# A graph network kernel on one core: constant products in TensorE's pauses, the first load in halves, the last group finished in pairs

## The chip, the core and the metric

The kernel runs on one core of a Trainium2 chip. A core has five engines that run their own instruction streams in order and meet at semaphores: TensorE (PE in the profile; its weight loads are the row PEld), VectorE (DVE), ScalarE (ACT), GpSimd (POOL) and SyncE (SP), which here only issues DMAs. The metric is device time in microseconds (us) of one execution; lower is better. The kernel before took 2499.52 us, the median of three runs (2499.09 to 2500.66).

## The reference

The inputs are x, 128 graphs ("batches") of 128 nodes with 256 features, and adj, their 128x128 adjacency matrices. Four layers follow each other, each wrapped as `x = layernorm(x + layer(x, adj))`:

- Layer 0 is a gated graph network of three steps. A step computes `m = h @ weight[i]`, sums the messages over the graph, `aggr = adj^T @ m`, and updates the state with a GRU cell: `gi = aggr @ w_ih.T + b_ih`, `gh = h @ w_hh.T + b_hh`, two sigmoid gates, one tanh candidate.
- Layers 1, 2 and 3 are graph attention: `Wh = x @ W.T`, scores `e[i,j] = leaky(a1.Wh[i] + a2.Wh[j])`, masked by adj, softmax over j, and `out = attention @ Wh`. Layer 2 gives 0 where a row has no neighbour.

All of it is float32.

## The kernel before

**Tiling.** The 128 batches are taken in 32 groups of 4 (`G = 4`, `NG = 32`). A tile has 128 partitions; the state of a group is two tiles of 128 features by 512 columns (4 batches of 128 nodes). `gru(g, stage)` (L675) does layer 0 for group g, `gat(g, ...)` (L838) the three attention layers.

**Layer 0.** The products of the GRU cell are done in Strassen's form with seven block products per gate pair (`strassen`, L631); its matmuls (L649) accumulate in five PSUM banks with the tag "gate". They multiply tiles with two constant weight tables: `whs`, made from w_hh, and `wcs[i]`, made at the start of each step's first use from `weight[i]` and w_ih (`input_weights`, L452: matmuls at L465, evictions by `scale`, seven block sums L429 to L435). All other PSUM results go through three banks with the tag "bank". For groups 0 and 1 the input is transposed by TensorE (`transposed`, L546, matmuls L554); for later groups by DMA (`turned`, L500: a copy that splits 32-bit words into 16-bit halves, L404 or L406, a DMA transpose L516, and a copy that joins them, L510). Steps 1 and 2 split the state into three bfloat16 parts (`thirds`, L521, subtractions at L536).

**Attention layers.** Scores are dot products on VectorE with an accumulator (L850); masked rows with their maximum at L885; leaky ReLU, exp and row sums on ScalarE (L889, L906); the attention matrix is transposed and multiplied (L956), evicted, and multiplied by the weights (L967); L973 adds the residual on VectorE, one instruction per batch, two batches per PSUM bank. The layernorm of these layers is `deviation` (L586): per batch a square with a sum on ScalarE (L590), then one small VectorE instruction for all four batches (L594 in the first attention layer, L601 later), then `power` (L560), a GpSimd instruction that raises 128x4 numbers to -0.5 (L563). After the last layer four ScalarE instructions scale the four batches (L980) and one DMA of 512 KB writes the group out (L982).

**What sets the order.** The program is unrolled. A planner (`Plan`, L51) gets every operation with assumed durations per engine that may do it (for instance `{"ACT": 475, "DVE": 602}`), its reads and writes, a priority by group and stage, and the pools of buffers; it places operations one after the other by a list schedule, repeats this with due times worked back from the result (`latest`, L125), seven passes in all, and keeps the pass with the shortest planned span (`order`, L102). It decides the order on each engine, which engine does an operation that may run on two or three, and the buffer slot. `LATER` (L342) shifts the stages of different groups against each other, so that layer 0 of some groups runs beside the attention of others; the last four groups (`LAST = 4`, "the tail") are done by priority alone, and use TensorE transposes instead of DMA ones. Because of the planner a change of one operation can move instructions far away from it.

**The start.** VectorE zeroes three small tiles "f" (L369), which later hold scores. SP issues the loads in this order: x of group 0 (xs, 512 KB, L681), its adj (am, 256 KB, L682), weight[0] (256 KB), w_ih (2 x 384 KB, L424), x of group 1 (512 KB), w_hh (2 x 384 KB), adj of groups 1 to 4, and x of group 2, which takes over the buffer of group 0's x. TensorE does, in this order: 8 transposes of group 0's x, 16 products with its adj (L719), 4 transposes of group 1's x, the products for `wcs[0]` (L465), 4 more, and then the gate products.

Of the kernel before, what the change touches and what calls it, by code (L numbers as in the profile page):

```python
# [16 lines left out]
P = 128  # L17
# [291 lines left out]
def adj_resnorm_kernel(  # L309
# [30 lines left out]
    U16, BF16 = mybir.dt.uint16, mybir.dt.bfloat16  # L340
    BOTH = ("DVE", "POOL")
    LATER = (0.25, 1.75, -0.5, -0.25, 0.25, -1.0)  # L342
    plan = Plan({t: n for t, (n, _) in tags.items()}, own)
# [24 lines left out]
    for t in slots["f"]:  # L368
        nc.vector.memset(t, 0.0)  # L369

# [31 lines left out]
    def copy(e, dst, src):  # L402
        if e == "ACT":
            nc.scalar.copy(dst, src)  # L404
        else:
            nc.vector.tensor_copy(dst, src)  # L406
# [138 lines left out]

    def transposed(src, src_of, prio):  # L546

        res = []
        for c in range(KC):
            b_, dst = bank(), Buf("k2", GN)  # L550

            def fn(e, b_=b_, c=c):
                for b in range(G):
                    nc.tensor.transpose(T(b_)[:, b * P:(b + 1) * P], src_of(b, c), ident)  # L554
            plan.op({"PE": 437}, fn, reads=[src], writes=[b_], prio=prio)
            plan.op(EVICT, lambda e, b_=b_, dst=dst: copy(e, T(dst), T(b_)), reads=[b_], writes=[dst], prio=prio)
            res.append(dst)
        return res

    def power(ve, prio):  # L560

        rstd = Buf("v", G)
        plan.op({"POOL": 980}, lambda e: nc.gpsimd.tensor_tensor(T(rstd), T(ve), neghalf, ALU.pow),  # L563
                reads=[ve], writes=[rstd], prio=prio, port=BOTH, holds=False)
        return rstd
# [19 lines left out]

    def deviation(y, before, prio):  # L586

        ss, ve = Buf("v", G), Buf("v", G)
        for b in range(G):
            plan.op({"ACT": 400}, lambda e, b=b: nc.scalar.activation(  # L590
                next(nobody[0]), T(y)[:, b, :], AF.Square, accum_out=T(ss)[:, b:b + 1]),
                reads=[(y, b)], writes=[(ss, b)], prio=prio, lag=85)
        if before is None:
            plan.op({"DVE": 78}, lambda e: nc.vector.tensor_scalar(  # L594
                T(ve), T(ss), 1.0 / D, EPS, op0=ALU.mult, op1=ALU.add),
                reads=[(ss, b) for b in range(G)], writes=[ve], prio=prio, port=BOTH)
        else:
# [3 lines left out]
            plan.op({"DVE": 78}, lambda e: nc.vector.scalar_tensor_tensor(  # L601
                T(ve), T(ss), 1.0 / D, T(eps), op0=ALU.mult, op1=ALU.add),
                reads=[(ss, b) for b in range(G)] + [eps], writes=[ve], prio=prio, port=BOTH)
        return ve
# [26 lines left out]
    def strassen(gates, kept, prio):  # L631
# [41 lines left out]
        return o0, o1, bx  # L673

    def gru(g, stage):  # L675

# [16 lines left out]
        if g < 2:  # L693
            hT = transposed(xs, lambda b, c: T(xs)[:, b, c * P:(c + 1) * P], prio)
# [8 lines left out]
        for i in range(STEPS):  # L703
# [4 lines left out]
            for c in range(KC):  # L708
# [11 lines left out]
                if by_thirds and h is not None:  # L720
                    plan.op({"PE": 12 * 55.6 + 56}, fn, reads=[low, h[0][c], h[0][2]], writes=[b_], prio=prio, room=[a_, t])
                else:
                    plan.op({"PE": 4 * 222.7}, fn, reads=[am, xs if h is None else h[c]], writes=[b_], prio=prio, room=[a_, t])
                agg.append(a_)
# [113 lines left out]
    def gat(g, xc, no, stage):  # L838
# [3 lines left out]
        for l in range(3):  # L842
# [118 lines left out]
            for b0 in range(0, G, 2):  # L961
# [9 lines left out]
                for b in (b0, b0 + 1):  # L971
# [4 lines left out]
                            reads=[b_, rden, (xc, b)], writes=[(y, b)], prio=prio)  # L976
            xc, ve = y, deviation(y, ve, prio)
            rstd = power(ve, prio)
        for b in range(G):
            plan.op({"ACT": 400}, lambda e, b=b: nc.scalar.mul(T(xc)[:, b, :], T(xc)[:, b, :], T(rstd)[:, b:b + 1]),  # L980
                    reads=[(xc, b), rstd], writes=[(xc, b)], prio=prio)
        plan.op({"SP": 60}, lambda e: nc.sync.dma_start(out[g * G:(g + 1) * G].rearrange("b n d -> n b d"), T(xc)),  # L982
                reads=[(xc, b) for b in range(G)], prio=prio)

# [57 lines left out]
```

## Time and profile before

| | |
|---|---|
| runs | 2499.09, 2499.52, 2500.66 us |
| the profiled execution | 2499.94 us, of which the instructions span 2497.9 us |
| instructions in the profile | 42545 |
| TensorE busy | 2469.1 us, 99% |
| VectorE busy | 2164.0 us, 87% |
| ScalarE busy | 1925.7 us, 77% |
| GpSimd busy | 781.9 us, 31% |
| share of 16 DMA engines that the main queue used | 29.9% |
| mean granted TensorE clock | 0.997 |

The profile is of one execution. "Busy" of TensorE has modelled ends: a matmul is given its whole latency (0.38 us for 128 columns by 256), while the next one starts 0.216 us after it, so a busy TensorE may still have lost time between two starts. Rows of the timeline read: start, length, engine, line, operation, output<-inputs, shapes, count, and in brackets how long the engine was idle before and what ended that. Rows of a window read: from and to, its length, the busy time of each engine with its number of instructions, the granted TensorE clock (1.00 is full speed), the share of the DMA engines and GB/s. Where the profile has no record of the clock the row shows 1.00.

### The profile page before, as it was taken

The numbers are of one execution on the slowest core, as the hardware profiler recorded it, in microseconds if no ns is written. First come the engines' busy times: TensorE is split into PE (matmuls) and PEld (weight loads), VectorE is DVE, ScalarE is ACT, GpSimd is POOL, SyncE is SP. The second block draws the span as 40 slices with busy tenths as digits, with TensorE's granted clock in tenths as the row PEclk, the third lists the DMA queues.
The fourth block names the chain that finished last, engine by engine and source line by source line (L and its number), as shares of the span: only waits on it lengthen the run. The fifth ranks groups of instructions, "written<-read, shape, count | busy, mean of one in ns | idle before, by whom it ended". The sixth has DMA issues, their size and how long they took to land.

```text
span 2497.9 us, 42545 instructions
## 1 busy us (share of the span) xinstructions
PE 2469.1 (99%) x13492; PEld 2180.1 (87%) x13492; DVE 2164.0 (87%) x6461; ACT 1925.7 (77%) x4835; POOL 781.9 (31%) x999
## 2 busy tenths in 40 slices
PE   8999999999999999999999999999999999999998
PEld 7888888888888888888888888888888888888877
DVE  6789888989888988889988889988889988877797
ACT  6578777888778787788887778887787888666577
POOL 2232233422334332334333334233333332211001
PEclk9999999999999999999999999999999999999999
DMA  5223233233333332333242233333233333110101
GB/s 148 56 56 64 60 76 69 64 81 60 76 64 73 72 81 60 73 68 73 68 77 68 61 80 68 73 71 74 60 77 68 76 65 68 26 39 18 38 1 35
DMA packets 456609, 161.38 MB, mean 65 GB/s; under 512 B 389184, under 2 KB 454720, under 8 KB 456384
## 3 DMA queue, kind: packets, MB, share of 16 engines
q1 hardware_dynamic: 455952, 158.65, 29.9%
q8 instruction: 106, 1.74, 0.3%
q14 instruction: 119, 0.97, 0.1%
q10 hardware_dynamic: 432, 0.01, 0.0%
HBM read 45.89 MB, written 16.78 MB: 25 GB/s over the span
## 4 chain that ended last, share of the span: by engine, by line
PE 86%; DVE 6%; ACT 4%; DMA 2%; issue 1%; POOL 0%; POOLq 0%; ACTq 0%; DVEq 0%
PE gate L649 63%; PE bank L967 10%; PE bank L956 6%; PE bank L716 3%; PE bank L719 2%; DVE nobody L850 2%; DMA k<-k 1%; DVE k L973 1%; ACT k L906 1%; ACT k L404 1%; DMA xs<-in_x_dram 1%; ACT k L510 1%; DVE k L406 1%; DVE k L654 1%; PE bank L822 0%
## 5 line engine op out<-in xcount | busy, mean ns | idle before, releaser
L649 PE MATMUL gate<-k,whs 128*128 128x256 f32 x4032 | 1205.2, 381 | 3.5 <-ACT k L742 1.6
L649 PE MATMUL gate<-k,wcs 128*128 128x256 f32 x4032 | 1199.3, 379 | 1.3 <-ACT wcs L404 1.3
L649 PEld LDWEIGHTS gate<-k,wcs 128*128 128x128 f32 x4032 | 766.0, 190 | 105.8 <-ACT wcs L404 1.8
L649 PEld LDWEIGHTS gate<-k,whs 128*128 128x128 f32 x4032 | 741.2, 190 | 107.8 <-ACT k L742 9.6
L654 DVE TENSOR_TENSOR k<-gate,k 128x512 f32<-128x512 f32 x576 | 388.4, 685 | 125.6 <-PE gate L649 80.4
L563 POOL TENSOR_TENSOR v<-v,neghalf 128x4 f32<-128x4 f32 x128 | 159.3, 1244 | 843.5 <-DVE v L601 460.9
L967 PE MATMUL bank<-gwT,k 128*128 128x256 f32 x1536 | 349.6, 380 | 1.6 <-DVE k L406 0.8
L967 PEld LDWEIGHTS bank<-gwT,k 128*128 128x128 f32 x1536 | 290.1, 190 | 43.7 <-DVE k L406 3.6
L850 DVE SCALAR_TENSOR_TENSOR nobody<-k,wa 128x256 bf16<-128x256 f32 x768 | 297.7, 427 | 0.7 <-ACT k L582 0.7
L753 ACT ACTIVATE k<-k,brz 128x256 f32<-128x256 f32 (+1 forms) x384 | 229.6, 624 | 71.1 <-DVE k L654 71.0
L618 POOL TENSOR_TENSOR k<-k,k 128x256 f32<-128x256 f32 x272 | 232.9, 867 | 104.1 <-DVE k L792 37.9
L404 ACT COPY k<-bank 128x512 f32<-128x512 f32 (+1 forms) x272 | 155.1, 572 | 112.0 <-PE bank L956 56.3
L735 ACT COPY k<-gate 128x512 f32<-128x512 f32 x288 | 167.9, 584 | 87.2 <-PE gate L649 83.7
L536 POOL TENSOR_TENSOR k<-k 128x512 f32<-128x512 f32 (+1 forms) x143 | 155.9, 1090 | 239.1 <-DVE k L792 189.4
L404 ACT COPY k<-k 128x512 bf16<-128x512 bf16 (+1 forms) x265 | 175.7, 694 | 53.8 <-DVE k L792 27.3
L869 POOL PARTITION_BROADCAST k<-k x336 | 138.4, 512 | 240.3 <-DVE k L406 149.1
L590 ACT ACTIVATE nobody<-k 128x256 bf16<-128x256 f32 x384 | 157.0, 415 | 60.5 <-DVE k L973 60.3
L510 ACT COPY k<-k 128x1024 uint16<-128x1024 uint16 x163 | 189.9, 1166 | 17.1 <-DMA k<-k 15.2
L956 PEld LDWEIGHTS bank<-k,k 128*128 128x128 f32 x1536 | 183.8, 192 | 11.0 <-DVE k L918 3.7
L956 PE MATMUL bank<-k,k 128*128 128x128 f32 x1536 | 190.2, 277 | 2.4 <-ACT k L510 1.5
L782 ACT ACTIVATE k<-k,bi 128x512 f32<-128x512 f32 x192 | 136.6, 726 | 66.4 <-DVE k L779 52.5
L973 DVE SCALAR_TENSOR_TENSOR k<-bank,v,k 128x256 f32<-128x256 f32 x384 | 166.9, 476 | 23.0 <-PE bank L967 22.8
(110 smaller groups left out, 3296.7 us busy)
## 6 DMA issues: line engine op xcount, KB each, us to landing
xs<-in_x_dram SPq DMA_DIRECT2D x32, 512.0 KB, 3.9
k<-in_x_dram SPq DMA_DIRECT2D x32, 512.0 KB, 4.1
out_dram<-k SPq DMA_DIRECT2D x32, 512.0 KB, 2.9
am<-in_adj_dram SPq DMA_DIRECT2D x32, 256.0 KB, 4.2
k<-k SPq DMA_TRANSPOSE x366, 3.1
k<-in_gnn_wT_dram SPq DMA_DIRECT2D x3, 256.0 KB, 4.7
k<-in_w_ihT_dram SPq DMA_DIRECT2D x2, 384.0 KB, 5.7
k<-in_w_hhT_dram SPq DMA_DIRECT2D x2, 384.0 KB, 6.7
```

Source lines behind the costliest of these rows:

```text
L404: nc.scalar.copy(dst, src)
L510: nc.scalar.copy(flat().bitcast(U16).rearrange("p (q h) -> p q h", h=2), T(rows).bitcast(U16).rearrange("p (h q) -> p q h", h=2))
L563: plan.op({"POOL": 980}, lambda e: nc.gpsimd.tensor_tensor(T(rstd), T(ve), neghalf, ALU.pow), reads=[ve], writes=[rstd], prio=prio, port=B ...
L618: nc.vector if e == "DVE" else nc.gpsimd).tensor_tensor(T(t)[:, j, :], a(), b(), ALU.subtract),
L649: nc.tensor.matmul(T(dst)[:, j * H:(j + 1) * H], T(w)[:, m, gt, :], moving(m, ms)[1](), start=first and n == 0, stop=n == len(todo) - 1, s ...
L654: plan.op({"DVE": 602}, lambda e: nc.vector.tensor_add(T(o)[:, :, j * H:(j + 1) * H], T(b_).rearrange("p (g n) -> p g n", g=2), T(part).re ...
L735: plan.op({"ACT": 475}, lambda e: nc.scalar.copy(T(dst), T(src)), reads=[src], writes=[(dst, 0), (dst, 1)], prio=prio)
L753: nc.scalar.activation(T(o)[:, gt, n0:n1], src(), AF.Tanh, bias=brz[:, gt * KC + c:gt * KC + c + 1], scale=0.5)
L850: plan.op({"DVE": 345}, lambda e, b=b, h=h, l=l, side=side, xc=xc: nc.vector.scalar_tensor_tensor(next(nobody[1]), T(xc)[:, b, :], 1.0, T( ...
L956: nc.tensor.matmul(T(b_)[:, b * P:(b + 1) * P], T(xc)[:, b, c * P:(c + 1) * P], T(pT)[:, b, :], start=True, stop=True)
L967: nc.tensor.matmul(T(b_)[:, (b - b0) * D:(b - b0 + 1) * D], T(aT[k])[:, b * P:(b + 1) * P], T(gwT)[:, l, k, :], start=(k == 0), stop=(k == ...
L973: nc.vector.scalar_tensor_tensor(T(y)[:, b, :], T(b_)[:, (b - b0) * D:(b - b0 + 1) * D], T(rden)[:, b:b + 1], T(xc)[:, b, :], op0=ALU.mult ...
```

## The change

There are four parts.

1. **Eight products at the start.** The tiles "f" are filled with 1.0 instead of 0.0, and before anything else TensorE multiplies the first of them with itself eight times (`idle_product`, 128x128 float32) into a gate bank. Nobody reads the result.
2. **Products in planned pauses.** After planning, the kernel walks over TensorE's operations in planned order. Where the plan has a pause of more than 1200 ns and there is a gate bank with no user left, it puts one or more such products ahead of the next operation: (pause - 1200) / 437 rounded down, plus one. In the built program that makes three places, all after the last gate product: four products ahead of the first transpose L822, three more behind it, and one ahead of the last pair of L956.
3. **The first x in halves.** For group 0 the load of x is two DMAs of two batches (256 KB) each, and `transposed` is done in two parts that need one half each. The transposes of the two halves go to the same two banks; the evictions and all later users wait for both.
4. **The last group ends in pairs.** In the last attention layer of the last group, `deviation` and `power` work on two batches at a time, the squares and the last scaling may run on VectorE as well as on ScalarE, and each pair is written out by a DMA of its own (256 KB).

The planner runs with these operations, so the order on all engines can differ from before everywhere.

```diff
+    FILL = 1200
...
     for t in slots["f"]:
-        nc.vector.memset(t, 0.0)
+        nc.vector.memset(t, 1.0)
...
+        for b0, b1 in parts:
+            for c in range(KC):
+                def fn(e, b_=res[c][0], c=c, b0=b0, b1=b1):
+                    for b in range(b0, b1):
+                        nc.tensor.transpose(T(b_)[:, b * P:(b + 1) * P], src_of(b, c), ident)
+                plan.op({"PE": 109 * (b1 - b0)}, fn, reads=[(src, b0)], writes=[(res[c][0], b0)], prio=prio)
...
+        for b0, b1 in parts:
+            plan.op({"POOL": 980}, lambda e, b0=b0, b1=b1: nc.gpsimd.tensor_tensor(
+                T(rstd)[:, b0:b1], T(ve)[:, b0:b1], neghalf[:, b0:b1], ALU.pow),
+                reads=[(ve, b0)], writes=[(rstd, b0)], prio=prio, port=BOTH, holds=False)
...
+    def square(e, y, b, ss):
+        if e == "ACT":
+            nc.scalar.activation(next(nobody[0]), T(y)[:, b, :], AF.Square, accum_out=T(ss)[:, b:b + 1])
+        else:
+            nc.vector.scalar_tensor_tensor(next(nobody[1]), T(y)[:, b, :], 1.0, T(y)[:, b, :], op0=ALU.mult, op1=ALU.mult,
+                                           accum_out=T(ss)[:, b:b + 1])
...
+        engines = {"ACT": 400} if parts == WHOLE else {"ACT": 400, "DVE": 345}
...
+    def idle_product(dst, n):
+
+        for _ in range(n):
+            nc.tensor.matmul(dst[:, 0:P], slots["f"][0], slots["f"][0], start=True, stop=True)
...
-        plan.op({"SP": 450}, lambda e: nc.sync.dma_start(T(xs), x_g), writes=[xs], prio=prio)
+        x_parts = ((0, 2), (2, G)) if g == 0 else ((0, G),)
+        for b0, b1 in x_parts:
+            plan.op({"SP": 450}, lambda e, b0=b0, b1=b1: nc.sync.dma_start(T(xs)[:, b0:b1], x_g[:, b0:b1]),
+                    writes=[(xs, b0)], prio=prio)
...
+            parts = ((0, 2), (2, G)) if g == NG - 1 and l == 2 else WHOLE
+            xc, ve = y, deviation(y, ve, prio, parts)
+            rstd = power(ve, prio, parts)
+        for b0, b1 in parts:
+            for b in range(b0, b1):
+                plan.op({"ACT": 400} if parts == WHOLE else {"ACT": 400, "DVE": 340}, lambda e, b=b: scale(
+                    e, T(xc)[:, b, :], T(xc)[:, b, :], T(rstd)[:, b:b + 1]),
+                    reads=[(xc, b), (rstd, b0)], writes=[(xc, b)], prio=prio, port=("DVE", "POOL") if parts != WHOLE else ())
+            plan.op({"SP": 60}, lambda e, b0=b0, b1=b1: nc.sync.dma_start(
+                out[g * G + b0:g * G + b1].rearrange("b n d -> n b d"), T(xc)[:, b0:b1]),
+                reads=[(xc, b) for b in range(b0, b1)], prio=prio)
...
     order = plan.order()
+    filled, ends, uses = {}, None, {}
+    for n, o in enumerate(order):
+        for b in o.bufs:
+            if b.tag == "gate":
+                uses[b.slot] = n
+    for n, o in enumerate(order):
+        if o.engine == "PE":
+            gap = o.start - ends if ends is not None else 0
+            ends = o.start + o.engines["PE"]
+            over = min(uses, key=uses.get)
+            if gap > FILL and uses[over] < n:
+                filled[o] = over, int((gap - FILL) // 437) + 1
...
+        idle_product(slots["gate"][0], 8)
         nc.gpsimd.load_library(library_config.all_libraries[10])
         for o in order:
+            if o in filled:
+                idle_product(slots["gate"][filled[o][0]], filled[o][1])
             o.fn(o.engine)
```

More of the change, by code (lines that the diff above doesn't have):

```diff
@@ L544, in thirds, with transposed @@
         return rows, lambda c, b, j: wide(where(c, j)[0])[:, where(c, j)[1], b * P:(b + 1) * P]
-    def transposed(src, src_of, prio):
+    def transposed(src, src_of, prio, parts):
         res = []
@@ L550, in transposed, with power @@
             b_, dst = bank(), Buf("k2", GN)
[L552 to L560, printed above, removed]
+            res.append((b_, dst))
+        for b0, b1 in parts:
[4 more added lines that the diff above has]
+                plan.op({"PE": 109 * (b1 - b0)}, fn, reads=[(src, b0)], writes=[(res[c][0], b0)], prio=prio)
+        for b_, dst in res:
+            plan.op(EVICT, lambda e, b_=b_, dst=dst: copy(e, T(dst), T(b_)), reads=[(b_, b0) for b0, _ in parts],
+                    writes=[dst], prio=prio)
+        return [dst for _, dst in res]
+    WHOLE = ((0, G),)
+    def power(ve, prio, parts=WHOLE):
         rstd = Buf("v", G)
-        plan.op({"POOL": 980}, lambda e: nc.gpsimd.tensor_tensor(T(rstd), T(ve), neghalf, ALU.pow),
-                reads=[ve], writes=[rstd], prio=prio, port=BOTH, holds=False)
+        for b0, b1 in parts:
+            plan.op({"POOL": 980}, lambda e, b0=b0, b1=b1: nc.gpsimd.tensor_tensor(
+                T(rstd)[:, b0:b1], T(ve)[:, b0:b1], neghalf[:, b0:b1], ALU.pow),
+                reads=[(ve, b0)], writes=[(rstd, b0)], prio=prio, port=BOTH, holds=False)
         return rstd
@@ L584, in layernorm, with deviation @@
                 reads=[(y, b), shift, rstd], writes=[(dst, b)], prio=prio)
-    def deviation(y, before, prio):
+    def square(e, y, b, ss):
[4 more added lines that the diff above has]
+                                           accum_out=T(ss)[:, b:b + 1])
+    def deviation(y, before, prio, parts=WHOLE):
         ss, ve = Buf("v", G), Buf("v", G)
+        engines = {"ACT": 400} if parts == WHOLE else {"ACT": 400, "DVE": 345}
         for b in range(G):
[L590 to L597, printed above, removed]
+            plan.op(engines, lambda e, b=b: square(e, y, b, ss),
+                    reads=[(y, b)], writes=[(ss, b)], prio=prio, lag=85, port=("DVE", "POOL") if parts != WHOLE else ())
+        if before is not None:
             eps = Buf("v", G)
@@ L600, in deviation @@
                     reads=[before], writes=[eps], prio=prio, port=BOTH)
-            plan.op({"DVE": 78}, lambda e: nc.vector.scalar_tensor_tensor(
-                T(ve), T(ss), 1.0 / D, T(eps), op0=ALU.mult, op1=ALU.add),
-                reads=[(ss, b) for b in range(G)] + [eps], writes=[ve], prio=prio, port=BOTH)
+        for b0, b1 in parts:
+            sums_of = [(ss, b) for b in range(b0, b1)]
+            if before is None:
+                plan.op({"DVE": 78}, lambda e, b0=b0, b1=b1: nc.vector.tensor_scalar(
+                    T(ve)[:, b0:b1], T(ss)[:, b0:b1], 1.0 / D, EPS, op0=ALU.mult, op1=ALU.add),
+                    reads=sums_of, writes=[(ve, b0)], prio=prio, port=BOTH)
+            else:
+                plan.op({"DVE": 78}, lambda e, b0=b0, b1=b1: nc.vector.scalar_tensor_tensor(
+                    T(ve)[:, b0:b1], T(ss)[:, b0:b1], 1.0 / D, T(eps)[:, b0:b1], op0=ALU.mult, op1=ALU.add),
+                    reads=sums_of + [eps], writes=[(ve, b0)], prio=prio, port=BOTH)
         return ve
@@ L693, in gru @@
         if g < 2:
-            hT = transposed(xs, lambda b, c: T(xs)[:, b, c * P:(c + 1) * P], prio)
+            hT = transposed(xs, lambda b, c: T(xs)[:, b, c * P:(c + 1) * P], prio, x_parts)
         else:
@@ L722, in gru @@
                 else:
-                    plan.op({"PE": 4 * 222.7}, fn, reads=[am, xs if h is None else h[c]], writes=[b_], prio=prio, room=[a_, t])
+                    plan.op({"PE": 4 * 222.7}, fn, reads=[am] + ([(xs, b0) for b0, _ in x_parts] if h is None else [h[c]]), writes=[b_], prio=prio, room=[a_, t])
                 agg.append(a_)
@@ L976, in gat @@
                             reads=[b_, rden, (xc, b)], writes=[(y, b)], prio=prio)
[L977 to L983, printed above, removed]
+            parts = ((0, 2), (2, G)) if g == NG - 1 and l == 2 else WHOLE
+            xc, ve = y, deviation(y, ve, prio, parts)
+            rstd = power(ve, prio, parts)
+        for b0, b1 in parts:
+            for b in range(b0, b1):
[5 more added lines that the diff above has]
+                reads=[(xc, b) for b in range(b0, b1)], prio=prio)
     def stage(g, n):
```

## The prediction

> **What bounds the kernel.** I read the page's busy row first, then windows by stage, then the timeline of the start and of the end.
>
> ```profile
> PE 2469.1 (99%) x13492; PEld 2180.1 (87%) x13492; DVE 2164.0 (87%) x6461; ACT 1925.7 (77%) x4835; POOL 781.9 (31%) x999
> ```
>
> Ninety-nine percent is an average over stages. Windows:
>
> ```profile
> 0.00:20.00 20.00, 13.61 (x55) 10.44 (x56) 12.03 (x32) 10.44 (x18) 3.57 (x10) 1.00 0.81 253
> 20.00:2399.00 2379.00, 2373.50 (x12953) 2099.01 (x12954) 2069.06 (x5998) 1838.29 (x4519) 764.38 (x976) 1.00 0.31 65
> 2399.00:2410.00 11.00, 6.85 (x31) 5.36 (x30) 10.73 (x48) 7.51 (x28) 0.00 (x0) 0.69 0.00 1
> 2410.00:2472.00 62.00, 58.91 (x372) 51.80 (x370) 61.89 (x352) 52.96 (x217) 9.95 (x9) 1.00 0.01 1
> 2472.00:2490.00 18.00, 16.22 (x89) 13.49 (x88) 9.75 (x35) 13.91 (x50) 3.02 (x3) 1.00 0.25 85
> ```
>
> The columns are PE, PEld, DVE, ACT, POOL, clock, DMA. From 20 to 2399 us TensorE is the bound (idle 5.5 us). From 2399 to 2472 it is VectorE: idle 0.3 us in 11 and 0.1 us in 62. The last 26 us are a chain through TensorE, ScalarE and GpSimd. So three small stages are edited, and the long one only passes on what it is given.
>
> The start, from the timeline:
>
> ```profile
> 4.98 1.94 PE L554 MATMUL bank<-ident,xs 128*128 128x128 f32 x8 [4.98 <-DMA xs<-in_x_dram]
> 6.71 3.62 PE L719 MATMUL bank<-am,xs 128*128 128x128 f32 x16
> 10.39 0.63 PE L554 MATMUL bank<-ident,xs 128*128 128x128 f32 x4
> 17.37 1.99 ACT L404 COPY k<-xs 128x1024 uint16<-128x1024 uint16 x2 [1.34 <-DMA xs<-in_x_dram]
> 19.27 0.51 ACT L404 COPY wcs<-k 128x384 f32<-128x384 f32 x1
> 19.82 0.70 PE L649 MATMUL gate<-k,wcs 128*128 128x256 f32 x2 [1.35 <-ACT wcs L404]
> ```
>
> To see: the 24 products to 10.1 us run at half pace. Sixteen take 3.62 us, (3.62 - 0.42) / 15 = 0.213 us each, where sixteen L956 of the same shape take 1.95 us in the tail, 0.112 each. (The clock column's 1.00 is no record here.) But what starts next at 10.39 is the transpose of group 1's x: that load is issued at 3.35 and takes 6.9 us to land, 10.26. And TensorE then waits until 19.82 for a piece of `wcs[0]`, which ScalarE copies at 19.27, behind two copies of group 2's x, which landed at 17.3.
>
> **Part by part.** The sum is made against the profiled execution's own 2499.94 us; it stands 0.42 above the median.
>
> *Eight products and x in halves.* The products cost 8 x 0.213 = 1.7 us from about 1.4 us (f zeroed at 0.82 to 1.27), in front of a load: nothing; if that cover went they would cost 1.7. The loads run back to back at 310 to 400 GB/s, so half the x lands 256 KB / 0.35 = 0.75 us earlier, about 4.1, the second at 4.84 as now. Four transposes then run early and the last four end at about 5.8 instead of 6.7. Each later load is issued one slot (0.45 us) behind, SP's queue being moved back by one, but the DMA engines are full from 3 to 17 us (share 1.0 to 1.2), so landings stay: am 5.8, group 1's x 10.26, group 2's x 17.3. VectorE turns am into floats in 0.43 us, so the adj products start at about 6.4 instead of 6.7 and end at 8.2 (fast clock) to 9.8 (half). Either way TensorE's next instruction, in the changed order too, is the transpose that waits for 10.26. Gain at 10.39: zero; late next is group 1's x. Downstream the changed order is different. On ScalarE the two evictions that finish `wcs[0]`'s second half (L410, 0.6 + 0.4) now stand between the two copies of group 2's x, and VectorE makes the piece that TensorE waits for: 17.37 + 1.0 (copy) + 1.0 (evictions) + 0.1 + 0.54 (copy, 128x384) + 0.1 = 20.1. Against 19.82: **+0.3**. Bounds: -1.35 if that wait vanished, +1.7 if the clock falls in a wait of 1.8 us and half of a 3.4 us stretch is lost. I take +0.3, worked out from rows.
>
> [...]
>
> *Products in the pauses.* Windows around the first pause of the tail:
>
> ```profile
> 2399.60:2403.00 3.40, 1.13 (x4) 0.68 (x4) 3.40 (x13) 1.96 (x5) 0.00 (x0) 1.00 0.01 2
> 2403.00:2406.40 3.40, 1.87 (x8) 1.48 (x9) 3.35 (x12) 2.26 (x9) 0.00 (x0) 0.51 0.00 0
> 2406.40:2409.80 3.40, 3.28 (x15) 2.88 (x16) 3.18 (x22) 2.73 (x11) 0.00 (x0) 0.50 0.00 0
> ```
>
> TensorE is idle for 2.25 us, and then granted half the clock for 6.8 us. In that time it runs about 32 products of 0.21 instead of 0.11 us, 3.2 us of its time, but VectorE is busy 3.35 and 3.18 of 3.40, so 0.05 + 0.22 = 0.27 us is all that a fast TensorE can hand on; the rest is hidden by VectorE's queue. The four products raise the busy time of the first window from 1.13 to about 1.6, 47%. Rows with a clock that fell: 1.13 of 3.4, 33%. A row that kept it: 2.2 of 3.4 (2460.9 to 2464.3, with a pause of 1.2 us). So about even odds. They wait for nothing (gate bank and f are old), and the next writer of that f comes several microseconds later. Cost, if they are late: 7 x 0.11 = 0.8, hidden by the 2.25 and 1.09 us pauses. Between -0.5 and +0.3, I take **-0.2**. The single product near the end, 0.11 us, sits in a pause of 0.46: 0.
>
> [...]
>
> *The end in pairs.*
>
> ```profile
> 2489.46 0.87 DVE L973 SCALAR_TENSOR_TENSOR k<-bank,v,k 128x256 f32<-128x256 f32 x2 [0.92 <-PE bank L967]
> 2490.04 0.42 ACT L590 ACTIVATE nobody<-k 128x256 bf16<-128x256 f32 x1 [0.95 <-DVE k L973]
> 2490.98 0.16 DVE L601 SCALAR_TENSOR_TENSOR v<-v,v 128x4 f32<-128x4 f32 x1 [0.64 <-ACT nobody L590]
> 2491.22 1.01 POOL L563 TENSOR_TENSOR v<-v,neghalf 128x4 f32<-128x4 f32 x1 [5.24 <-DVE v L601]
> 2492.26 1.70 ACT L980 ACTIVATE k<-k,v 128x256 f32<-128x256 f32 x4 [1.31 <-POOL v L563]
> 2493.99 0.37 SPq L982 DMA_DIRECT2D out_dram<-k  x1
> ```
>
> Squares: VectorE takes the last one, but in its order it has a scaling of the first pair before the small instruction of the second: 2490.27 + 0.42 (square, as L850) + 0.3 (scaling, L412) = 2490.98, the same as now. Gain 0; late there is VectorE's own queue. Power: the first pair's (its L973 end at 2488.5) runs at 2489.2 to 2490.2, free; the second's takes 1.01 as now, or half if it went by its two columns: gain 0 to 0.5, I take 0 (a GpSimd subtraction of 512 columns takes 1.09 and of 256 columns 0.87, so most is fixed). Scaling: behind the last power stand one instruction on ScalarE and one on VectorE, 0.5 instead of 1.70: **-1.2**. Output: the last DMA has 256 KB instead of 512; the old one took 2.9 us to land, and at 350 GB/s the half saves 0.75 (bounds 0 and 1.45, half of all): **-0.75**. The extra DMA issue (0.37, SP) lies at about 2491.1, ahead of the last. Sum of the end: -1.95.
>
> *The planner.* The changed program, put in order, holds the same work in the tail: from the last gate product on VectorE's and ScalarE's orders equal the old ones up to the last pairs. Before that they differ nearly everywhere. Counted by the rows' means, VectorE gets 26 us less and ScalarE 27 us more of 2000, which frees or binds neither; GpSimd gets 44 more of the subtractions L536 (187 of 224). TensorE's products are the same. What it loses between starts, by the trace's starts and counts: 9624 products of 256 columns x 0.216, 2476 float32 of 128 x 0.112, 1344 bfloat16 x 0.056 and 48 of L465 make about 2446 us of the 2489 to the last product; 43 are lost, of which some 9 at the start, 14 in the tail and 20 scattered. The scattered 20 can be dealt anew. Mean 0; by its spread over 24 slices of 100 us (0.1 to 2.3 us each), about 3 us either way.
>
> Sum: 2499.94 + 0.3 - 0.2 - 1.95 + 0 = 2498.1, and 0.42 less against the median: **2497.6 us**. 0.2% is 5 us, about what a measurement of this kernel can tell from no change.
>
> **Rivals.**
>
> 1. *A new deal of the long stage loses.* Place: L536 and the subtractions behind it, 44 of which go from VectorE (0.73 to 0.95) to GpSimd (1.05 to 1.12) and delay the state of the next step. Price: 0.25 us for each that TensorE comes to wait for; all 44 would be 11 us, 2508.6. From 28 on it passes 5 us over the old time. For it: TensorE has waited for ScalarE's copies of such results (1.6 us at L742). Against: idle of only 5.5 us in 2379 shows slack almost everywhere.
> 2. *It wins.* The scattered 20 shrink by a quarter or more, or the start's wait goes too (-1.35): 2492 to 2494. For it: 26 us less on VectorE; against: TensorE's idle gives little to win.
> 3. *The end does not gain*, the change doing there what it says but no more: the second power waits behind VectorE's scaling, or two small DMAs land no sooner than one (half DMAs not at 350 GB/s): 2499.5.
>
> **How the numbers follow.** Forecast 0.58, its own range 2494.6 to 2500.6 (3 us either way). Rival 1 0.12, rival 2 0.21, rival 3 0.09. The range goes from 2493.2 (rival 2's middle) to 2503.5, between rival 3 and the point where rival 1 counts. Faster by over 0.2% 0.21, slower 0.12, within 0.67 (forecast and rival 3).
>
> **What would show it.** At the start: products of f at 0.213 us from about 1.4; group 1's transpose still at 10.4; the wait for `wcs[0]` ending at about 20.1. In the tail: VectorE's busy 62 of 62 whatever the clock does behind the first pause. At the end: the last output issued 1.2 us sooner after the last product, landing in about 2.2 us. Wrong would be: a landing of group 1's x well before 10.26; idle TensorE between 20 and 2399 other than 5.5 us by more than 3; a VectorE in the tail with less work.

## The result, and the profile after

The changed kernel took **2502.75 us** (median of 21 runs, 2499.80 to 2505.46) against 2499.58 us for the kernel before on the same chip (21 runs, 2498.94 to 2501.03): a ratio of 1.0013, with an interval of 1.0007 to 1.0019. It is slower by about 3.2 us, where 2.0 us of gain were predicted. The range (2493.2 to 2503.5) holds the time, the direction is wrong.

The profiled execution of after took 2505.46 us, the slowest of its runs (span 2503.4), that of before 2499.94 (span 2497.9). So the two traces lie 5.5 us apart where the medians lie 3.2 apart.

The page of after, busy row and the chain that ended last:

```profile
PE 2475.2 (99%) x13524; PEld 2184.0 (87%) x13524; DVE 2164.0 (86%) x6429; ACT 1950.3 (78%) x4895; POOL 779.6 (31%) x997
PE 72%; DVE 12%; ACT 10%; DMA 3%; issue 2%; POOL 0%; POOLq 0%; ACTq 0%; SPq 0%; DVEq 0%
```

ScalarE has 24.6 us more work than before and VectorE none less in sum. In the chain TensorE's share was 86% before; of the 14 points that it lost, VectorE and ScalarE took six each.

Two windows of after, with the columns of the prediction (PE, PEld, DVE, ACT, POOL, clock, DMA):

```profile
20.00:2399.00 2379.00, 2369.26 (x12916) 2093.16 (x12917) 2065.55 (x5949) 1858.53 (x4568) 761.37 (x973) 1.00 0.31 65
2410.00:2472.00 62.00, 56.77 (x348) 49.97 (x349) 60.88 (x341) 50.25 (x204) 8.80 (x8) 0.97 0.01 1
```

The first row is the one to read: TensorE's idle time in the long stage went from 5.5 to 2379.00 - 2369.26 = 9.7 us. The tail starts some 7 us later than before, which the second row does not allow for.

The start of after, from the timeline:

```profile
1.04 3.78 PE L697 MATMUL gate<-f 128*128 128x128 f32 x16 [1.04 <-DVE f L370]
4.61 1.70 PE L558 MATMUL bank<-ident,xs 128*128 128x128 f32 x8
6.27 2.05 PE L746 MATMUL bank<-am,xs 128*128 128x128 f32 x16
10.76 0.63 PE L558 MATMUL bank<-ident,xs 128*128 128x128 f32 x4 [2.44 <-DMA xs<-in_x_dram]
19.50 0.55 DVE L407 COPY wcs<-k 128x384 f32<-128x384 f32 x1 [2.96 <-ACT k L411]
20.11 0.70 PE L668 MATMUL gate<-k,wcs 128*128 128x256 f32 x2 [1.30 <-DVE wcs L407]
```

Behind the constant products (L697) the 16 products with adj (L746, before L719) take 2.05 us instead of 3.62: (2.05 - 0.42) / 15 = 0.109 us each instead of 0.213, the pace of the tail (0.112). Each of the eight is two matmuls in the profile, so the row says x16, and they take 3.78 us. TensorE then stands for 2.44 us until group 1's x lands, and its next transpose starts at 10.76 instead of 10.39. The product that waits for the piece of `wcs[0]` made by VectorE starts at 20.11.

The end of after:

```profile
2497.26 0.88 DVE L1000 SCALAR_TENSOR_TENSOR k<-bank,v,k 128x256 f32<-128x256 f32 x2
2498.53 0.35 DVE L413 TENSOR_SCALAR k<-k,v 128x256 f32<-128x256 f32 x1
2498.79 0.15 DVE L620 SCALAR_TENSOR_TENSOR v<-v,v 128x2 f32<-128x2 f32 x1
2499.02 0.70 POOL L571 TENSOR_TENSOR v<-v,neghalf 128x2 f32<-128x2 f32 x1 [1.09 <-DVE v L620]
2499.76 0.51 ACT L411 ACTIVATE k<-k,v 128x256 f32<-128x256 f32 x1 [1.07 <-POOL v L571]
```

VectorE's scaling of the first pair (L413) does stand ahead of the small instruction L620, as foreseen. The power over two columns takes 0.70 us where four took 1.01.

Laid over each other, with the products of the gates (L649, after L668) as milestones, the traces split the 5.5 us like this:

| stretch | after minus before, us | how it is worked out |
|---|---|---|
| start, to the first gate product | +0.33 | 16.49 - 16.16 |
| long stage, first to last gate product | +6.92 | last one at 2408.06 and 2400.81, less 0.33 |
| tail, to the last product | +0.61 | 89.16 - 88.55 |
| end, last product to the end of the span | -2.30 | 6.22 - 8.52 |

The edits themselves are in the first, third and fourth rows. The loss is in the second, where no line of the long stage was edited.

### The profile page after: what moved, and what is told of

It is laid out like the page before. It is cut to its first block, busy times and chain, and to the rows that moved or that the text cites. A ratio compares the mean times of both kernels' runs of the same rounds, so it can differ in the third digit from the quotient of the medians.

```text
span 2503.4 us, 42495 instructions
## 1 busy us (share of the span) xinstructions
PE 2475.2 (99%) x13524; PEld 2184.0 (87%) x13524; DVE 2164.0 (86%) x6429; ACT 1950.3 (78%) x4895; POOL 779.6 (31%) x997
## 4 chain that ended last, share of the span: by engine, by line
PE 72%; DVE 12%; ACT 10%; DMA 3%; issue 2%; POOL 0%; POOLq 0%; ACTq 0%; SPq 0%; DVEq 0%
PE gate L668 52%; PE bank L994 9%; PE bank L983 5%; PE bank L743 3%; DVE nobody L877 2%; DMA k<-k 2%; PE bank L746 2%; ACT k L405 2%; DVE k L673 2%; ACT k L933 2%; DVE k L407 1%; ACT k L511 1%; ACT k L780 1%; DVE k L1000 1%; ACT k L762 1%
## 5 line engine op out<-in xcount | busy, mean ns | idle before, releaser
L668 PE MATMUL gate<-k,whs 128*128 128x256 f32 x4032 | 1206.9, 381 | 5.5 <-DVE k L673 2.6
L668 PE MATMUL gate<-k,wcs 128*128 128x256 f32 x4032 | 1199.2, 379 | 1.3 <-DVE wcs L407 1.3
L668 PEld LDWEIGHTS gate<-k,wcs 128*128 128x128 f32 x4032 | 766.0, 190 | 105.7 <-DVE wcs L407 1.7
L668 PEld LDWEIGHTS gate<-k,whs 128*128 128x128 f32 x4032 | 738.9, 190 | 114.1 <-ACT k L769 12.4
L673 DVE TENSOR_TENSOR k<-gate,k 128x512 f32<-128x512 f32 x576 | 392.3, 685 | 112.9 <-PE gate L668 83.9
L571 POOL TENSOR_TENSOR v<-v,neghalf 128x4 f32<-128x4 f32 x129 | 143.6, 1113 | 923.1 <-DVE v L620 565.1
L405 ACT COPY k<-k 128x512 bf16<-128x512 bf16 (+1 forms) x304 | 217.8, 738 | 85.4 <-DVE k L819 59.9
L780 ACT ACTIVATE k<-k,brz 128x256 f32<-128x256 f32 (+1 forms) x384 | 224.4, 623 | 66.4 <-DVE k L673 66.3
L537 POOL TENSOR_TENSOR k<-k 128x512 bf16<-128x512 f32 (+1 forms) x187 | 203.8, 1092 | 173.4 <-DVE k L819 71.3
L896 POOL PARTITION_BROADCAST k<-k x336 | 152.1, 553 | 315.5 <-ACT k L405 241.0
L637 POOL TENSOR_TENSOR k<-k,k 128x256 f32<-128x256 f32 x246 | 200.3, 829 | 148.3 <-ACT k L411 59.2
```

The source lines that it names most:

```text
L537: nc.vector if e == "DVE" else nc.gpsimd).tensor_tensor(out(), T(whole), top(), ALU.subtract),
L637: nc.vector if e == "DVE" else nc.gpsimd).tensor_tensor(T(t)[:, j, :], a(), b(), ALU.subtract),
L668: nc.tensor.matmul(T(dst)[:, j * H:(j + 1) * H], T(w)[:, m, gt, :], moving(m, ms)[1](), start=first and n == 0, stop=n == len(todo) - 1, s ...
L673: plan.op({"DVE": 602}, lambda e: nc.vector.tensor_add(T(o)[:, :, j * H:(j + 1) * H], T(b_).rearrange("p (g n) -> p g n", g=2), T(part).re ...
L780: nc.scalar.activation(T(o)[:, gt, n0:n1], src(), AF.Tanh, bias=brz[:, gt * KC + c:gt * KC + c + 1], scale=0.5)
```

## The experiments

The comparison gives a first theory. **Theory A:** the planner answers the split first load with another deal, that is another order, another buffer for many tiles and another engine for many operations of the long stage, and this deal costs about 5 us; the edits alone gain 2 to 3. Its rivals: the halves themselves cost (later loads, lost clock), or the products in pauses do. Each kernel below ran beside the kernel before on its chip, which had medians of 2499.09 to 2499.47.

### Parts alone, and with the order held

All parts but the halves. The planner then gives exactly the old order up to the new end:

```diff
-        x_parts = ((0, 2), (2, G)) if g == 0 else ((0, G),)
+        x_parts = ((0, G),)
```

> All of the change except the halves of the first x. The order of all other instructions is then that of the kernel before. Theory A (the halves made the planner deal the long stage anew, and that deal costs TensorE some 4 to 7 us): 2499.6 - 2.3 (the end, as the profile after shows it: 6.2 us instead of 8.5 from the last product to the end) - 0 to 0.5 = 2497 us, ratio 0.999. Theory B (the products in the pauses, or the end's extra instructions, cost the time): 2501 us or more. Last gate product at 2400.8 us as before by A, 2404 or later by B.

Measured: 2496.74, ratio 0.9989 (0.9980 to 0.9997). The rest of the change gains 2.6 us.

All parts with the halves, but told to the planner as one load of the old cost, with the transposes of the first x put in the order of the halves inside its two operations. The order of everything else is the old one:

```diff
-        x_parts = ((0, 2), (2, G)) if g == 0 else ((0, G),)
+        x_parts = ((0, G),)
...
+            def load_x(e, b0=b0, b1=b1):
+                for n0, n1 in ((0, 2), (2, G)) if g == 0 else ((b0, b1),):
+                    nc.sync.dma_start(T(xs)[:, n0:n1], x_g[:, n0:n1])
+            plan.op({"SP": 450}, load_x, writes=[(xs, b0)], prio=prio)
```

> All of the change, but the planner sees one load and one transposition as before; the two half loads and the transposes by halves are issued where it placed these. Theory A (the order alone costs): 2497 us like the kernel with a whole first x, at most 0.4 more for group 1's x landing later. Theory C (the halves themselves cost, by the extra DMA issue and a clock that falls in the 2.4 us wait for group 1's x): 2501 us or more with the old order too, lost before 30 us.

Measured: 2496.06, ratio 0.9986 (0.9977 to 0.9995). Two DMAs in place of one cost nothing here (2496.06 against 2496.74 with one). What they trigger in the planner does.

The halves alone, without products and pairs; the planner deals as for the changed kernel (this extract and the next show what is added to a kernel with none of the parts):

```diff
-        x_parts = ((0, G),)
+        x_parts = ((0, 2), (2, G)) if g == 0 else ((0, G),)
```

> Only the first x in halves, with the order that the planner then makes; no constant products, no pairs. Theory A: the changed kernel's median plus the 2.3 us of its end, 2505 us (2503 to 2507), last gate product 4 to 7 us later than before. Theories B and D (the halves are harmless, another part costs): 2499.6.

Measured: 2504.15, ratio 1.0020 (1.0011 to 1.0029), the loss without any gain.

The constant products alone, at the start and in the pauses, in the old order:

```diff
+        idle_product(slots["gate"][0], 8)
...
+            if o in filled:
+                idle_product(slots["gate"][filled[o][0]], filled[o][1])
```

> Only the constant products (start and pauses), in the old order, no halves, no pairs. Theory A: 2499.6 - 0.2, between 2499.0 and 2500. Theory B (they cost, by holding the next product or through the clock): 2501 or more. At the start the adj products run at 0.11 us each instead of 0.213 and TensorE then waits about 2 us for group 1's x, which starts at 10.4 as before.

Measured: 2498.73, ratio 0.9997 (0.9988 to 1.0006): nothing that can be told from zero. The pairs at the end are then worth 2498.73 - 2496.74 = 2.0 us.

### The deal without any edit

The next kernel is the one before with one number of the planner changed, so that it finds the new pattern for exactly the old work:

```diff
-        plan.op({"SP": 450}, lambda e: nc.sync.dma_start(T(xs), x_g), writes=[xs], prio=prio)
+        plan.op({"SP": 900 if g == 0 else 450}, lambda e: nc.sync.dma_start(T(xs), x_g), writes=[xs], prio=prio)
```

> The kernel before with one number changed: the cost that the planner assumes for the first load of x on SP, 900 in place of 450. No instruction is added, removed or split; the planner answers with a deal of the pattern that the changed kernel has: 187 of the 224 subtractions of the thirds on GpSimd (before: 143). Theory (the new deal of the long stage costs some 5 us by itself): 2504, ratio 1.001 to 1.003. Rival (new deal and halves cost only together, because the halves land at other times than the planner thinks): 2499.3, ratio 1.000. Rival (any new deal is as likely above as below, the pattern says nothing): anything from 2494 to 2506.

Measured: 2503.19, ratio 1.0018 (1.0009 to 1.0027). Same instructions, other order: +3.9 us. Theory A stands, and no edit is needed for the loss.

With 500 in place of 900 the planner finds a third deal:

> As the run with 900, with 500 as the assumed cost of the first load of x. The planner answers with a third pattern: 131 of the 224 subtractions on GpSimd, 93 on VectorE. Theory, where the pattern with 187 is what costs: 2499.5, ratio 0.999 to 1.001. Rival (every departure from the old deal costs, since the old one was the one that was kept): 2502 or more. Rival (luck of any deal): anything from 2494 to 2506.

Measured: 2497.14, ratio 0.9991 (0.9982 to 0.9999). A new deal can also gain; a departure from the old one does not cost as such.

### Is it the engine, or the order?

The first rival of the prediction put the price on 44 subtractions (L536) that go from VectorE to GpSimd. That can be tried with the old order held:

```diff
     order = plan.order()
+    for o, e in zip(subtractions, "PPDDPPPP..."):
+        o.engine = {"P": "POOL", "D": "DVE"}[e]
```

> The kernel before, every instruction in its old place in the common order, but each of the 224 subtractions of the thirds is issued on the engine that the new deal gave it: 187 on GpSimd (143 before). Theory that these subtractions carry the loss (the prediction's first rival: 44 more of them on GpSimd, each up to 0.25 us later): 2503 to 2505. Theory that the loss lies in the order in which the engines take the rest, not in who subtracts: 2499.3, within 1 us. If late subtractions cost even more where the order was not made for them: above 2505.

Measured: 2501.35, ratio 1.0008 (0.9999 to 1.0017). At +2.1 it lies between the two theories, and its interval just reaches 1.

> The converse: the kernel with only the halved first load and so the new order (2504.15 measured), but each of the 224 subtractions of the thirds on the engine that it had before (143 on GpSimd, 81 on VectorE). Theory that the subtractions carry the loss: back to 2499 to 2500. Theory that the order carries it: 2504 again, within 1 us, or above it because VectorE, at 87% in the long stage, gets 44 subtractions of some 0.6 us more at places planned without them.

Measured: 2506.97, ratio 1.0029 (1.0018 to 1.0040). Giving VectorE its 44 subtractions back in the new order does not bring the time back, it costs 2.8 us more. So putting them back does not repair the new order. But neither run changes the engine alone: each puts work on an engine at a place planned for another, and the next three runs show that this costs by itself. What the subtractions carry of the loss stays open.

Then the same for everything that more than one engine may do, and for the copies alone (edit as above, over 1,903 and 1,239 operations):

> The kernel before with every instruction at its old place in the common order and in its old buffer, but each of the 1,903 operations that more than one engine may do goes to the engine that the deal with 900 gave it (that deal measured 2503.19, ratio 1.0018). Theory S (the share of the engines is what costs: fewer copies and subtractions on VectorE, more on ScalarE and GpSimd): 2503, ratio 1.001 to 1.003, at least the 2501.35 that the subtractions alone gave. Theory O (the order and the buffers cost, not the share): 2499.3 to 2501.4, no more than with the subtractions alone. Above 2505 if work is put on an engine at a place that was planned for another.

> As the run with the whole new share, for the copies and scalings alone that ScalarE or VectorE may do (1,239 operations; 186 go from VectorE to ScalarE, 153 the other way); the subtractions and sums stay where they were. Theory S: 2501 to 2502, so that copies and subtractions (+2.1) make the whole of +4. Theory O: 2499.3, within 1 us.

> The converse: order and buffers of the deal with 900 (2503.19), each of the 1,903 operations on the engine that it had before. Theory S: back to 2499 to 2500. Theory O: 2503 or more. Neither, but a deal whose order and share belong together: above 2505, as the run with the new order and the old subtractions (2506.97) suggests.

Measured: 2571.20 (ratio 1.0288, 1.0274 to 1.0302), 2557.13 (1.0232, 1.0218 to 1.0246) and 2567.23 (1.0271, 1.0257 to 1.0285). All three are misses by some 55 to 70 us, for both theories. An operation given to another engine at a place planned for the first one is far worse than either deal. TensorE's waits in the second of them, from 100 to 2395 us (line, what it waited for: us, times, longest):

```profile
PE gate L649 <- ACT k L742: 19.5, 41, 1.7
PE gate L649 <- ACT k L735: 5.6, 17, 0.7
```

Share and order of a deal cannot be priced apart in this way. But the rows name a place where ScalarE hurts in this kernel: L735 and L742 are copies out of a gate's PSUM bank that the planner may give to ScalarE alone, and TensorE's next product into that bank waits for them.

### Pattern or luck?

That suggests **theory P**: the new pattern gives ScalarE more copies (656 by L404 instead of 626), it comes later to the gates' banks, and TensorE waits. Rival L: every deal has its own luck. Two more deals from other numbers of the first load, 1200 and 2000:

> The kernel before with the planner's assumed cost of the first load of x at 1200: again 187 of the 224 subtractions on GpSimd, 657 copies on ScalarE (before: 143 and 626), found from another number than 900. Theory P (deals of this pattern cost, whatever led to them): 2503, ratio 1.001 to 1.003. Rival L (each deal has its own luck, the pattern says nothing): from 2496 to 2505, as likely below 2501 as above.

Measured: 2506.39, ratio 1.0028 (1.0017 to 1.0039).

> The same with 2000: the planner comes back to a deal near the old one, 138 subtractions on GpSimd, 627 copies on ScalarE. Theory P: 2497 to 2500, ratio 0.999 to 1.0005. Rival L: from 2496 to 2505. If a larger assumed cost were itself what costs (it pushes work back at the start): above 2503.

Measured: 2499.50, ratio 1.0001 (0.9993 to 1.0010). The larger number gives the better time, since it leads back to the old pattern.

And two where the planner counts the copies of the thirds on ScalarE nearer to what the trace shows:

```diff
-    ROUND = {"ACT": 475, "DVE": 602}
+    ROUND = {"ACT": 650, "DVE": 602}
```

> The assumed load of 900 that led to the slow deal (2503.19), and one more number changed for the planner: a rounding copy of the thirds on ScalarE counted at 650 instead of 475 (the trace shows 0.696 us of mean before, 0.742 in the deal with 900). The deal now has 612 copies on ScalarE and 145 subtractions on GpSimd. Theory P, with the reason that ScalarE comes later to the banks of the gates because of its extra copies: 2498 to 2500, and its wait of the weight loads for the copies out of a gate's bank back to some 22 times, 10 us (35 times, 11 to 12 us in the slow deals). Rival L: from 2496 to 2508.

Measured: 2499.68, ratio 1.0002 (0.9993 to 1.0011).

> The same copy cost of 650 with the load as before (450): 613 copies on ScalarE, 146 subtractions on GpSimd, nearly the deal of the run beside it. Theory P: within 1.5 us of the run with 900 and 650, since the load's number does not change the pattern here. Rival L, or a price of the assumed load by itself: 3 us or more apart from it.

Measured: 2500.39, ratio 1.0004 (0.9996 to 1.0013).

All nine runs in one table. "Copies" are those by L404 on ScalarE, of all kinds, "subtractions" those of L536 on GpSimd (of 224). "Lost" is TensorE's time between starts beyond what the products need, from 100 to 2395 us, worked out from the starts with 0.216, 0.111 and 0.056 us for the three common shapes; "at gates" is the part of it that lies ahead of a gate product (L649). "Gate waits" are the printed waits of the weight loads of L649 in the same stretch, added up; a weight load can wait while TensorE still works on the products before it (before, 9.6 us of waits for L742 stand beside 1.6 us of TensorE's own), so they are not time lost.

| deal | subtractions | copies | lost, us | at gates, us | gate waits, us | median, us | ratio |
|---|---|---|---|---|---|---|---|
| load 500 | 131 | 633 | 14.9 | 8.0 | 9.6 | 2497.14 | 0.9991 |
| before | 143 | 626 | 18.8 | 10.5 | 11.7 | 2499.58 | 1 |
| load 2000 | 138 | 627 | 18.2 | 10.2 | 11.6 | 2499.50 | 1.0001 |
| load 900, copy 650 | 145 | 612 | 18.0 | 10.4 | 10.0 | 2499.68 | 1.0002 |
| load 450, copy 650 | 146 | 613 | 17.9 | 9.9 | 9.7 | 2500.39 | 1.0004 |
| after | 187 | 656 | 23.9 | 12.3 | 17.1 | 2502.75 | 1.0013 |
| load 900 | 187 | 656 | 22.3 | 11.5 | 16.2 | 2503.19 | 1.0018 |
| halves only | 187 | 656 | 23.0 | 12.7 | 17.5 | 2504.15 | 1.0020 |
| load 1200 | 187 | 657 | 21.8 | 12.3 | 16.8 | 2506.39 | 1.0028 |

The four runs of the one pattern are the four slow ones, and all four have 16 to 17.5 us of waits at the gates; the other five have 9.6 to 11.7. But the nine runs are not nine deals. Laid side by side (operation, tiles and shape of each instruction in turn), the traces of 900 and 1200 have TensorE's 13,492 instructions in the same order without exception and 4,899 of ScalarE's 4,900; after and the halves alone differ from 900 in some sixty places of 25,000. Before and 2000 are nearly one order in the same way, and so are the two with the copy at 650. So there are four orders, one of them slow. The slow one is slow in four kernels, whatever led to it; whether its pattern makes it so, or whether this one order is unlucky (rival L), four orders cannot tell.

The reason that theory P gives can be followed further, in the waits of TensorE's weight loads, 100 to 2395 us (what was waited for: us in total, times, longest us). Before:

```profile
PEld gate L649 <- ACT k L742: 9.6, 22, 1.1
```

After (L769 is L742, L673 is L654):

```profile
PEld gate L668 <- ACT k L769: 12.4, 35, 0.9
PEld gate L668 <- DVE k L673: 2.3, 7, 0.6
```

The deal with 900, no edit:

```profile
PEld gate L649 <- ACT k L742: 11.3, 35, 0.7
```

The deal with 900 and the copy at 650:

```profile
PEld gate L649 <- DVE k L654: 5.9, 13, 1.2
PEld gate L649 <- ACT k L742: 1.3, 3, 0.8
```

In the slow pattern the weight loads wait for the copy out of a gate's bank 35 times instead of 22. With fewer copies on ScalarE that falls to 3 times, far below the 22 that were expected, and VectorE's additions at the gates (L654) take part of its place, 13 times.

The other side is ScalarE's own idle time, in its groups of instructions: busy us and mean ns of one, then idle us ahead of them and what ended it. The copies of the thirds and those at the gates, before:

```profile
L404 ACT COPY k<-k 128x512 bf16<-128x512 bf16 (+1 forms) x257 | 170.8, 696 | 52.0 <-DVE k L792 26.2 <-POOL k L536 24.0 <-DVE k L536 1.0
L735 ACT COPY k<-gate 128x512 f32<-128x512 f32 x277 | 161.4, 584 | 85.0 <-PE gate L649 81.6 <-issue 1.0
L739 ACT ACTIVATE k<-gate,bhn 128x256 f32<-128x256 f32 x277 | 132.4, 478 | 14.0 <-PE gate L649 13.8
```

The same groups of after:

```profile
L405 ACT COPY k<-k 128x512 bf16<-128x512 bf16 (+1 forms) x296 | 212.8, 741 | 83.7 <-DVE k L819 59.0 <-DVE k L537 12.7 <-POOL k L537 11.4
L762 ACT COPY k<-gate 128x512 f32<-128x512 f32 x278 | 161.5, 581 | 59.8 <-PE gate L668 59.0
L766 ACT ACTIVATE k<-gate,bhn 128x256 f32<-128x256 f32 x276 | 131.9, 478 | 4.1 <-PE gate L668 3.7
```

The same groups in the deal with 900 and the copy at 650:

```profile
L404 ACT COPY k<-k 128x512 bf16<-128x512 bf16 (+1 forms) x277 | 200.0, 737 | 42.3 <-DVE k L792 36.4 <-POOL k L536 3.3 <-DVE k L536 1.0
L735 ACT COPY k<-gate 128x512 f32<-128x512 f32 x276 | 159.9, 581 | 86.5 <-PE gate L649 82.3 <-issue 1.7 <-PE bank L862 1.2
L739 ACT ACTIVATE k<-gate,bhn 128x256 f32<-128x256 f32 x278 | 132.0, 475 | 10.3 <-PE gate L649 8.8
```

Idle time of ScalarE that a gate product ends is slack: ScalarE stood ready when the product was done. In the slow pattern it shrinks from 81.6 to 59.0 us at the first copy and from 13.8 to 3.7 at the second, while the copies of the thirds grow by 39 instructions and 42 us. In the deal with the copy at 650 it is back, 82.3 and 8.8 us. That deal has fewer copies by L404 in all, but its copies of the thirds take 200.0 us, 29 more than before, at no loss. (Here "idle" is no loss.)

Against theory P as the whole reason stands the column "at gates". Of the 3.0 to 5.1 us that TensorE loses more in the slow order than before, 1.0 to 2.2 lie ahead of gate products; in the run with 900 it is 1.0 of 3.5. The rest lies ahead of the products of the attention layers and of the sums over the graph. So late copies at the gates can be at most a part of the loss, about a third in two of the four runs and just over half in the others; no run moved those copies alone, and why this order is slow stays open.

The slowest run of the slow order has a price of its own, at the start. Its traces lie 3.9 us behind those of 900, and 3.6 of that is there by 70 us. The wait for `wcs[0]` was 1.9 instead of 1.3 us, and then the clock fell for 3.41 us, where in the run with 900 it was full. From the run with 1200:

```profile
21.00:24.50 3.50, 3.50 (x10) 2.79 (x9) 1.26 (x3) 2.24 (x3) 0.00 (x0) 0.51 0.97 208
```

The gate products in this stretch end 1.7 us later for it.

### Do the gains add up?

> All parts of the change (constant products, first load in halves, last group in pairs), in the order that the planner gives when it is told one load at a cost of 500 (that order alone measured 2497.14, ratio 0.9991; all parts in the old order 2496.06, ratio 0.9986). If the gains of order and parts add up: 2494, ratio 0.9975 to 0.998. If the order of 500 gains by what the parts gain too: 2496, ratio 0.9986.

Measured: 2495.66, ratio 0.9984 (0.9975 to 0.9993). Parts (-3.2) and order (-2.1) would make -5.3; measured is -3.4, which at this resolution is the same as the parts in the old order (0.9986). Both beat both kernels. The simpler one is the latter: keep the change, and do not let the planner see the split.

## Why the prediction was wrong, point by point

- **The step that failed** is "The planner": "VectorE gets 26 us less and ScalarE 27 us more of 2000, which frees or binds neither", and from it "Mean 0; ... about 3 us either way". The new deal costs 3.9 us by itself (the run with 900) and 4.9 with the halves. An average load of 77% was taken as proof that ScalarE binds nothing, and for the mean of 0 no other reason was given. In the run with 900 ScalarE has 24.4 us more work, near the 27 that were counted, but VectorE only 3.8 less, not 26. The slack of ScalarE ahead of its copies at the gates went with it, yet only 1.0 of the 3.5 us that TensorE lost more lies at gate products. That the order costs is shown; by which waits is not.
- **Rival 1** (the new deal loses, 0.12) is what happened, with its sign and less than half its price. Its place is not settled. It named late subtractions on GpSimd. With them alone in the old order the loss was 2.1 us (interval -0.2 to +4.2) instead of up to 11; in the slow deal ScalarE's copies wait less for GpSimd's L536 than before (11.4 against 24.0 us). The row that it quoted, 1.6 us of TensorE's waits at L742, is a wait for a copy out of a gate's bank, not for a subtraction.
- **What would show it** did: idle TensorE in the long stage "other than 5.5 us by more than 3" was named as the sign, and it was 9.7.
- **Start, +0.3:** right in its sum and its path, with some luck in the terms. The wait for `wcs[0]` ended at 20.11 where 20.1 was worked out, and the first gate product came 0.33 later. But the landings did not stay: group 1's x landed at 10.63 instead of 10.26 (its transpose started at 10.76, not 10.4) and the first copy of group 2's x started at 17.65 instead of 17.37; the two evictions, 0.86 instead of 1.0 us, and the shorter gaps between the steps took that back. The eight products took 3.78 us, not 1.7, since each is two matmuls in the profile; the transposes behind them started at 4.61, though the first half had landed at 3.96, and that cost nothing, as TensorE had 2.44 us to wait after them. The 16 products with adj took 1.57 us less (2.05 for 3.62), and none of it came through: TensorE waited 2.44 us behind them. The bound of +1.7, a clock lost behind that wait, is what the run with 1200 met.
- **Pauses, -0.2:** not told from zero, as the size said (0.9997 for both sets of products). With them alone half clock lasted 3.41 instead of 6.83 us in the tail, and the stretch from the last gate product to the last product was still no shorter, 89.14 against 88.55 us. Where the clock was never lost there (all parts in the old order, granted 1.00 from 2399 to 2472 us) it took 87.86. So here a lost clock cost the tail more than the 0.27 us that VectorE's rows allowed, about 1.3 us between these two kernels with the same products. The trace shows where: with the fall at 2407.99 us, behind the pauses, VectorE waits 0.9 us for the products of L967 and 0.2 for those of L956 in the 16 us after the last gate product; with the clock kept it waits for nothing there, and before, with the fall at 2403.03, for 0.2 us. So in this kernel the products did not prevent the fall: it came 4.96 us later than before, at a place where VectorE had to wait for it. (The table's kernels without the products, all with 6.83 us of half clock, have 88.34 to 89.49 us for this stretch, so 0.6 us between two orders says little.) The seven products took 1.88 us, not 0.8, being fourteen matmuls, and stayed hidden: in after the transpose behind the first four starts 2.64 us after the last gate product, before 2.63.
- **End, -1.95:** right, term by term: 2.0 for the pairs by the runs, 2.3 in the trace, of which the last scaling has 1.19 (0.51 for 1.70 us) and what follows it to the end 0.73 (3.18 for 3.91). Of the 0.35 more, 0.31 is the power: 0.70 us for two columns, where 1.01 was taken and 0.5 was the far bound.
- **The sum:** for the edits -1.85 predicted, -2.6 (without the halves) and -3.2 (with them) measured in the old order (the prediction's terms make 2497.7, where it has 2497.6); for the deal 0 predicted, +3.9 to +4.9 measured, and +6.9 in the run that also lost the clock at its start.

## What to carry to other kernels

Where a list scheduler sets the order, an edit at the edge is two changes, the edit and a new deal of everything, and the second can be larger; make the deal alone (change an assumed cost, leave the work) and the edit alone (hold the order) before judging either. A mean load of 77% does not show that an engine can take more work for nothing: read the idle time ahead of the instructions that hand the bound engine its next buffer, and whether it is the bound engine that ends it. Here that idle time shrank in the slow order, which is a sign and not yet a price. And count orders, not runs: four kernels in one order are one sample of what an order costs. Moving an operation to another engine in an order planned for the first one is no test of that engine's load: it cost 58 to 72 us where whole deals differ by 9.

## What the runs showed of the hardware that was not expected

**The same work kept and lost the clock.** In the tail after the last gate product, the changed kernel and the one with all parts in the old order run the same instructions with the same pauses, to within 0.02 us. The timeline of after:

```profile
2408.28 1.05 PE L697 MATMUL gate<-f 128*128 128x128 f32 x8
2413.40 0.32 PE L906 MATMUL bank<-ident,f 128*128 128x128 f32 x1 [1.05 <-DVE nobody L877]
2415.41 3.48 PE L983 MATMUL bank<-k,k 128*128 128x128 f32 x16
```

And of all parts in the old order:

```profile
2399.99 1.05 PE L702 MATMUL gate<-f 128*128 128x128 f32 x8
2405.11 0.32 PE L913 MATMUL bank<-ident,f 128*128 128x128 f32 x1 [1.05 <-DVE nobody L884]
2407.11 2.05 PE L990 MATMUL bank<-k,k 128*128 128x128 f32 x16
```

Every start is 8.29 or 8.30 us earlier in the second, and yet sixteen products take 2.05 us there and 3.48 in the first, at a granted clock that falls at 2415.76 for 3.41 us. In the second the clock stays at 1.00 from 2399 to 2472 us. TensorE's longest pause between the first filled products and those sixteen is 1.36 us in both. Three more kernels have this tail: two lost the clock (all parts but the halves, 0.51 from 2408.1 to 2411.6 us, and the constant products alone, from 2407.99 us), one kept it (all parts in the order of 500, 1.00 from 2399 to 2472 us). So filling these pauses did not by itself decide whether the clock was kept; what did, no run shows.

**A lost clock at the start cost nothing in one kernel and 1.7 us in another.** With all parts in the old order the granted clock was 0.50 from 12.6 to 16.0 us and the first gate product came at 18.60 instead of 16.16. But the wait for `wcs[0]` (1.35 us before) was gone in return, and TensorE's lost time in the first 100 us was 8.4 us, as in the kernel with the whole first load. In the run with 1200 the fall came behind that wait, at 21.06 us, among the gate products, and they did not make up for it.

**The power on GpSimd is not mostly fixed cost.** The last one of the kernel took 1.01 us for 128x4 numbers before and 0.70 for 128x2 in after. By these two an estimate of the fixed part is 0.39 us (2 x 0.70 - 1.01).
